# Convolution layers 2 and 3 on row groups without halos: 64x64 and 32x32 products that join each group and its next

## The chip, the cores and the metric

The kernel runs on one core of one Trainium2 chip. The metric is the device time in microseconds (us) of one execution of the whole kernel. The engines are TensorE (PE, with PEld for its weight loads), VectorE (DVE), ScalarE (ACT), GpSimd (POOL) and SyncE (SP, which only issues DMAs). Each engine works through its own instructions in order and waits on semaphores for the others.

## The reference

Four residual layers act on x of shape (4, 8, 512, 512), float32. Each adds a branch of the group-normalised input, with 4 groups of 2 channels.

```python
x = x + _L0_conv_ref(_gn(x), ...)            # spiking attention with four projections
x = x + _L1_conv_ref(_gn(x), L1_conv_w)      # depthwise 13x13, reflected edges
x = x + _L2_conv_ref(_gn(x), L2_conv_weight, L2_conv_bias)
x = x + _L3_conv_ref(_gn(x), L3_conv_weight, L3_conv_bias)
```

The change concerns layers 2 and 3, both 3x3 convolutions from 8 to 8 channels with a border of zeros. Layer 2 rounds its input and its weights to integers of at most 127 before it convolves (the scale of the input is the largest absolute value of the whole normalised tensor), and divides by the scales afterwards. Layer 3 is a plain float32 convolution.

```python
sx = MAX_Q / jnp.max(jnp.abs(x))
qx = jnp.clip(jnp.round(x * sx), -MAX_Q, MAX_Q)      # the weights likewise, with sw
out = conv(qx, qw, padding=1) / (sx * sw) + bias     # layer 2
out = conv(x, weight, padding=1) + bias              # layer 3
```

The four images along the first axis are called t = 0 to 3 below; an image has 8 channels of 512 rows.

## The kernel before

Layers 0 and 1 come first and leave their result in DRAM, one tensor `x2d[t]` for each image. Its rows are image row by image row with the 8 channels of a row side by side, so that consecutive partitions hold row 0 channel 0, row 0 channel 1 and so on. Inside a row the 512 columns are stored by phase: first every fourth column from 0, then every fourth from 1, and so on (`PH` = 4 phases of `NV` = 128 columns). Layer 1 needed that order and layer 2 works in it: a step of one column is a step to the next phase, and only the outer two phases need a neighbour from another phase, which the padded tile `xq` of six phases holds.

Layers 2 and 3 (`layers23`) cut each image into 85 windows of 8 rows (`W_IN`), one every 6 rows (`W_STEP`). A window is 64 partitions, a tile two windows, a pair two tiles; an image has 22 pairs. The work of one step of the loop at the end is one pair:

- `load` brings a pair from DRAM, five steps ahead, with two DMAs on SP's queue.
- `normalise` (L1113, ACT) scales and shifts it, two steps ahead. `quantise` (L1125, DVE) rounds it to bf16 integers one step ahead, and POOL fills in the two padding phases (L1129, L1130).
- `layer2` runs three 128x128 products of 512 columns per tile (L1146, PE), one for each horizontal tap. `band2` holds the vertical taps as a banded matrix, with two corner blocks by which the two windows of a tile serve each other. DVE (L1153) takes the sum out of PSUM, scales it, adds the residual and writes it to `x3` in the natural order of columns, so with a step of four floats. ACT squares some tiles for the statistics of layer 3's group norm (L1160), DVE does the others (L1165).
- `halos` copies the rows at the windows' edges between the windows in `x3` by DMA (L1304), in four chunks per image and pair of windows, on SP's queue for the first image and on POOL's for the others.
- `norm3` makes the mean and deviation of the finished image and folds them into the weights `band_t`. It is a generator that is resumed twice a step, so that its pieces lie between the others. A mask leaves the windows' doubled rows out of the sums.
- `layer3` works on the image before, 22 + `LAG` = 25 steps behind layer 2. Each window takes three 64x64 float32 products (L1249, PE; each is two records in the profile); the four windows of a pair lie in four different quarters of the array. The residual is folded into the middle tap. ACT adds a constant and takes the result out of PSUM (L1258), and one DMA per tile on SP's queue stores 12 rows (L1265). Four banks of PSUM (`ps_r`) serve it, two per step.

The order on each engine is set by a scheduler, with hints: `tc.issue_after(op)` places what follows behind `op`. `weights23` builds the banded matrices out of the taps with short products (L951) while layer 1 runs. `x3` is a ring of 26 pairs.

Of the kernel before, what the change touches and what calls it, by code (L numbers as in the profile page):

```python
# [67 lines left out]
W_IN, W_STEP, W_ALL = 8, 6, 85  # L68
N_PAIRS = (W_ALL + 3) // 4
W2_N = 2 * N_PAIRS - 1  # L70
HALF = P // 2
LAG = 3
RING = 23 + LAG


def place(q):

    p, c = divmod(q, 4)
    return p, c // 2, (c % 2) ^ (c // 2)


def windows(k):

    p, j = divmod(k, 2)
    every = [(a, 4 * p + 2 * j + (a ^ j)) for a in range(2)]
    return [(a, q) for a, q in every if q < W_ALL]


def valid(q):

    return 0 if q == 0 else 1, W_IN if q == W_ALL - 1 else W_IN - 1
# [6 lines left out]
def shape_constants():  # L98
# [3 lines left out]
    mask2 = np.zeros((2, W_IN, B, W2_N, 2), np.float32)  # L102
    for k in range(W2_N):
        for a, q in windows(k):
            mask2[a, slice(*valid(q)), :, k] = 1
# [9 lines left out]
    for o in range(W1_OUT):  # L115
# [3 lines left out]
    c128 = np.concatenate(  # L119
        [block, same, ind, mask2.reshape(P, -1), eye.reshape(P, -1)], 1  # L120
    )

    c24 = np.zeros((3, B, 2 * W_IN + 1, B), np.float32)
    for dy in range(3):
        c24[dy, np.arange(B), W_IN - 1 + dy, np.arange(B)] = 1
    return c128, slide.reshape(K1, -1), c24.reshape(3 * B, -1)
# [3 lines left out]
def network(ctx: ExitStack, tc: tile.TileContext, i: dict, out: bass.AP):  # L130
# [19 lines left out]
    block, same, ind = part(P), part(P), part(G)  # L150
    mask2 = part(W2_N * 2)
# [58 lines left out]
    st1 = [const.tile([P, T, PAIR, NC, 2, 6], F32, name=f"st1_{g}") for g in range(G)]  # L210
# [14 lines left out]
    shared = first.enter_context(tc.tile_pool(name="shared", bufs=1))  # L225
    with ExitStack() as s:
        head = layer0(
            s, tc, i, x_in, x1d, ident, block, avg, group_stats, st1, norm1, band1d, r1, w_sum, shared
        )
# [3 lines left out]
    def pool(name, bufs=1, **where):  # L233
# [3 lines left out]
    st2 = late.tile([P, T, B, W1_N // 2 // N_PS1, 6], F32, name="st2")  # L237
# [4 lines left out]
        "x": ctx.enter_context(pool("x2", 9, side="right")),  # L242
        "y": ctx.enter_context(pool("y2", 2, side="right")),
        "o": ctx.enter_context(pool("o3", 10, side="right")),
    }
    with ExitStack() as s:
        ps_1 = s.enter_context(pool("ps_2", space=PSUM))
        layer1 = Layer1(
# [3 lines left out]
        for g in range(1, G):  # L252
            if g == 1:
                with ExitStack() as behind:
                    for op in layer1.started:
                        behind.enter_context(tc.issue_after(op))
                    norm1(G - 1, ps_1)
                    w23 = weights23(tc, i, late, early["y"], ps_1, ident)
# [3 lines left out]
    with ExitStack() as s:  # L262
        layers23(
            s, tc, x2d, out, ident, ind, mask2, avg_same, group_steps, m2, r2, most, w23, early, pool
        )
# [655 lines left out]
def weights23(tc, i, pool, scratch, ps_1, ident):  # L921
# [7 lines left out]
    n_taps = 3 * B  # L929
    w = {}  # L930
    parts = scratch.tile([P, 2, D], F32, tag="y", name="parts")
    c24 = parts[:n_taps, 0, : i["c24"].shape[1]]
    nc.scalar.dma_start(c24, i["c24"])
    w2, w3, below = (parts[:n_taps, 1, j * n_taps : (j + 1) * n_taps] for j in range(3))
    nc.scalar.dma_start(w2, i["w2"])
    nc.scalar.dma_start(w3, i["w3"])
    inner = parts[:, 1, P : P + 3 * HALF // 2].bitcast(BF16)
# [6 lines left out]
    def banded(taps, band, name, firsts):  # L944

        for b, first in enumerate(firsts):
            ps = ps_1.tile([P, W_IN, n_taps], F32, tag="misc", name=f"ps_{name}")
            for row in range(W_IN):
                at = (W_IN - first - row) * B
                for a in range(2):  # L950
                    nc.tensor.matmul(  # L951
                        ps[a * HALF : (a + 1) * HALF, row, :], lhsT=c24[:, at : at + HALF],
                        rhs=taps, start=True, stop=True,
                    )
            for dx in range(3):
                nc.vector.tensor_copy(
                    band[:, b, dx, :].rearrange("p (r c) -> p r c", c=B),
                    ps[:, :, dx * B : (dx + 1) * B],
                )
        return band  # L960

    band3 = pool.tile([P, 2, 3, HALF], F32, name="band3")
    w["band3"] = banded(w3, band3, "band3", (-1, 1))
    w["sum3"] = pool.tile([P, 2, HALF], F32, name="sum3")
    nc.vector.tensor_add(w["sum3"], band3[:, :, 0, :], band3[:, :, 1, :])
    nc.vector.tensor_add(w["sum3"], w["sum3"], band3[:, :, 2, :])
    w["eye3"] = pool.tile([P, 2, 3, HALF], F32, name="eye3")
    nc.vector.memset(w["eye3"], 0.0)  # L970
    nc.vector.tensor_add(
        w["eye3"][:, 0, 1, B:], ident[:, : HALF - B], ident[:, HALF : P - B]
    )
    nc.vector.tensor_add(
        w["eye3"][:, 1, 1, : HALF - B], ident[:, B:HALF], ident[:, HALF + B :]
    )

    wall = scratch.tile([P, 2, D], F32, tag="y", name="wall")
# [12 lines left out]
    w["band2"] = band2 = pool.tile([P, 2, 3, P], BF16, name="band2")  # L991
    nc.gpsimd.memset(band2, 0.0)
    inner = banded(w2, inner.rearrange("p (b x m) -> p b x m", b=1, x=3), "inner2", (0,))
    nc.vector.tensor_copy(below, w2)
    nc.vector.memset(below[: 2 * B, :], 0.0)
    ps = ps_1.tile([P, 2, n_taps], F32, tag="misc", name="ps_outer2")
    for a in range(2):
        half = slice(a * HALF, (a + 1) * HALF)
        at = (W_IN - W_STEP) * B
# [348 lines left out]
```

## Time and profile before

| what | value |
|---|---|
| median of 3 runs | 2902.83 us (2902.46 to 2903.03) |
| span of the profiled execution, first to last instruction | 2900.8 us |
| PE busy | 2818.8 us, 97% of the span |
| DVE, POOL, ACT busy | 2183.1, 868.8, 549.2 us |
| layers 2 and 3 | from about 2492 us to the end |
| layer 2 products (L1146) | 516 records, 131.5 us busy |
| layer 3 products (L1249) | 2040 records, 242.7 us busy |
| loads of layer 2, stores of layer 3 | 168 of 256 KB, 164 of 192 KB |

The profiled execution has no time of its own beside its span; the span is 2.0 us below the median of the runs. A group line in the profile names the source line, engine, operation, output<-inputs and shapes, then the count, the busy time and the mean length of one instruction; what follows is the idle time of the engine just before them and what ended it. Matmuls overlap, so their busy time is less than count times mean. A line of the chain of waits gives a start, a length and the instructions that the end of the program hung on in that stretch.

### The profile page before, as it was taken

The page shows a single profiled execution, that of the slowest core. Times are in us where ns is not written, and L with a number is a line of the kernel's source. Part 1 is how long each engine was busy: PE and PEld are TensorE (multiplying, and loading weights), DVE is VectorE, ACT ScalarE, POOL GpSimd, SP SyncE. Part 2 cuts the span into 40 slices and gives each one's busy share as a digit, 9 for nine tenths or more (in the row PEclk, how much of TensorE's full clock was granted, in tenths as well). Part 3 has the DMA queues.
Part 4 walks back from the last instruction along what each step waited for, and adds up shares of the span by engine and source line. Part 5 has one row for each costly group of instructions (what it writes and reads, how often), then busy time and mean ns, then how long its engine had stood idle before and what let it go on. Part 6 is the DMA issues. An engine that isn't in the chain of part 4 may idle for free. (4 is left out here: it accounts for less than half of the span.)

```text
span 2900.8 us, 36559 instructions
## 1 busy us (share of the span) xinstructions
PE 2818.8 (97%) x12868; PEld 1302.5 (45%) x12868; DVE 2183.1 (75%) x3888; ACT 549.2 (19%) x851; POOL 868.8 (30%) x1920
## 2 busy tenths in 40 slices
PE   7999999999999999999999999999999999689999
PEld 3444555545555545455555555445333333223334
DVE  6897788788779878878877886886665665888870
ACT  2200100011010001001000000110111121677774
POOL 2242243333234323333422343332311111232220
PEclk9899999999999999999999999999999999999999
DMA  8433222223222232222222122212877788699975
GB/s 209 115 89 76 59 67 67 74 74 74 59 67 67 77 76 68 59 67 67 75 67 51 45 59 52 52 45 75 221 203 207 209 219 224 157 201 234 224 191 148
DMA packets 326127, 324.01 MB, mean 112 GB/s; under 512 B 21519, under 2 KB 240439, under 8 KB 325831
## 3 DMA queue, kind: packets, MB, share of 16 engines
q1 hardware_dynamic: 263024, 239.48, 34.1%
q0 software_dynamic: 19776, 56.14, 6.0%
q10 hardware_dynamic: 43143, 26.05, 3.1%
q8 instruction: 101, 1.65, 0.3%
q14 instruction: 83, 0.68, 0.1%
HBM read 212.44 MB, written 103.65 MB: 109 GB/s over the span
## 5 line engine op out<-in xcount | busy, mean ns | idle before, releaser
L524 PE MATMUL ps_in<-w_v,xn 128*128 128x512 f32 x1024 | 459.1, 599 | 5.4 <-DVE w_v L359 5.4
L524 PE MATMUL ps_in<-w_kq,xn 128*128 128x512 f32 x1024 | 449.8, 592 | 0.0
L843 PE MATMUL ps_conv<-x,bt 112*64 112x512 f32 x2048 | 445.2, 592 | 0.1
L524 PE MATMUL ps_in<-xn,w_kq 128*128 128x512 f32 x1024 | 444.9, 592 | 0.0
L560 PE MATMUL ps_b<-toep,vtok 128*64 128x512 bf16 x3072 | 367.1, 383 | 0.4 <-DVE v_o L575 0.4
L475 ACT ACTIVATE h_q<-v_q,c_half 128x512 f32<-128x512 f32 x96 | 69.1, 721 | 1473.6 <-DVE v_q L471 893.9
L500 POOL TENSOR_TENSOR h_v<-h_v,c_v 128x512 f32<-128x512 f32 x96 | 121.8, 1269 | 728.0 <-DVE h_v L499 700.1
L587 PE MATMUL ps_out<-wp,so 128*128 128x512 f32 x1024 | 308.7, 444 | 0.0
L609 POOL COPY x1s<-x1s 128x2 f32<-128x2 f32 (+1 forms) x1024 | 226.6, 275 | 273.0 <-DVE x1s L598 273.0
L524 PEld LDWEIGHTS ps_in<-xn,w_kq 128*128 128x128 f32 x1024 | 194.3, 190 | 232.5 <-issue 220.4
L524 PEld LDWEIGHTS ps_in<-w_kq,xn 128*128 128x128 f32 x1024 | 194.3, 190 | 220.7 <-issue 206.2
L524 PEld LDWEIGHTS ps_in<-w_v,xn 128*128 128x128 f32 x1024 | 191.4, 191 | 222.9 <-issue 212.1
L843 PEld LDWEIGHTS ps_conv<-x,bt 112*64 112x64 f32 x2048 | 146.5, 135 | 288.0 <-issue 286.0
L560 PEld LDWEIGHTS <-vtok 128*64 128x64 bf16 x3072 | 176.1, 111 | 155.1 <-issue 5.6
L1249 PE MATMUL ps_conv<-x,band_t 64*64 64x512 f32 x2040 | 242.7, 595 | 0.0
L587 PEld LDWEIGHTS ps_out<-wp,so 128*128 128x128 f32 x1024 | 192.6, 188 | 94.0 <-issue 57.8
L1153 DVE SCALAR_TENSOR_TENSOR x<-ps_conv,inv,x 128x512 f32<-128x512 f32 (+1 forms) x172 | 186.1, 1169 | 46.9 <-PE ps_conv L1146 46.7
L598 DVE SCALAR_TENSOR_TENSOR x1s<-v_p,xr 128x256 f32<-128x256 f32 x256 | 187.6, 773 | 14.6 <-DMA x<-x1s 3.8
L865 POOL DMA_DIRECT2D x<-xo x128 | 71.4, 564 | 330.6 <-ACT xo L850 316.3
L850 ACT ACTIVATE xo<-ps_conv,off 128x512 f32<-128x512 f32 x128 | 87.6, 687 | 430.6 <-PE ps_conv L843 307.4
L500 POOL TENSOR_TENSOR h_k<-h_k,c_k 128x512 f32<-128x512 f32 x96 | 122.0, 1270 | 138.4 <-DVE h_k L499 138.4
L1146 PE MATMUL ps_conv<-xq,band 128*128 128x512 bf16 (+1 forms) x516 | 131.5, 391 | 31.3 <-POOL xq L1129 31.3
(193 smaller groups left out, 3113.8 us busy)
## 6 DMA issues: line engine op xcount, KB each, us to landing
x<-x SPq DMA_DIRECT2D x64, 917.0 KB
x<-x SPq DMA_DIRECT2D x168, 256.0 KB
x<-x1s POOLq DMA_DIRECT2D x128, 262.0 KB, 2.7
xq<-in_x SPq DMA_DIRECT2D x128, 256.0 KB
xr<-in_x SPq DMA_DIRECT2D x128, 256.0 KB
out<-o SPq DMA_DIRECT2D x164, 192.0 KB
xs<-in_x SPq DMA_DIRECT2D x112, 256.0 KB
x<-xo ACTq DMA_DIRECT2D x128, 128.0 KB
```

The lines of the kernel that those rows point to most:

```text
L500: nc.gpsimd.tensor_add(h, h, c_twice[n])
L524: mm = nc.tensor.matmul(ps, lhsT=lhsT, rhs=rhs, start=k == 0, stop=k == NC - 1)
L560: nc.tensor.matmul(pb[two * DH : (two + 1) * DH, :], lhsT=v[:, c, h * DH : (h + 1) * DH], rhs=toep[z][:, h, u : u + N], start=c == 0 and z ...
L587: nc.tensor.matmul(ps, lhsT=so[:, k, c * P : (c + 1) * P], rhs=wpT[z][:, k, :], start=k == 0 and z == 0, stop=k == NC - 1 and z == 1,)
L598: nc.vector.scalar_tensor_tensor(own, v.rearrange("p (g v) -> p g v", g=PH)[:, two, :], 1.0, by_phase[:, two, :], op0=ALU.is_ge, op1=ALU.add,)
L609: nc.gpsimd.tensor_copy(x1[:, f, u : u + n], x1[:, fm, um - n + 1 : um + 1][:, ::-1])
L843: mm = nc.tensor.matmul(ps[q * M1 : (q + 1) * M1, :], lhsT=bt[:, z, :], rhs=xt[:, w0 : w0 + N_PS1, z : z + NV], start=z == 0, stop=z == SH ...
L850: nc.scalar.activation(xo[:, a, :], ps, AF.Identity, bias=off[:, t : t + 1])
L865: engine.dma_start(bass.AP(dst.tensor, dst.offset + (q * n_half * W1_OUT * B + b) * D + f * NV, [[B * D, W1_OUT], [W1_OUT * B * D, n_half] ...
L1146: mm = nc.tensor.matmul(ps[:n_p, :], lhsT=w["band2"][:n_p, j, dx, :n_p], rhs=xq[:, j, dx : dx + PH, :], start=dx == 0, stop=dx == 2,)
L1153: done["DVE"] = nc.vector.scalar_tensor_tensor(own.rearrange("p (v g) -> p g v", g=PH), by_phase(ps[:n_p, :]), w["inv"][:n_p], by_phase(x[ ...
L1249: mm = nc.tensor.matmul(ps[j][b * HALF : (b + 1) * HALF, :], lhsT=band[half, b, dx, :], rhs=x3[half, s0 + j, dx : dx + D], start=dx == 0, ...
```

## The change

The windows go. An image is cut into 32 tiles of 16 rows (`W2_N` = 32); a tile is two octets of 8 rows (64 partitions) for layer 2 and four quads of 4 rows (32 partitions) for layer 3. A step of the loop prepares a pair of tiles, so an image has 17 steps (`N_PREP` = 17, the last of which has half a tile).

Layer 2: the input octet o holds rows 8o to 8o+6 and, in its last eight partitions, row 8o-1. Its output octet, rows 8o to 8o+7, then needs only its own input octet and the next one. So each output half takes three 64x64 products from its own input (opening) and three from the next (closing), and those of a tile are issued beside the opening ones of the tile after. The row that the eight partitions should hold for the residual, 8o+7, is loaded over row 8o-1 by two more DMAs on ACT's queue once `normalise` has read the tile. The DVE eviction reads and writes in phase order without a step; `x3` keeps six phases with padding, which POOL fills.

Layer 3: an output group is 4 rows, shifted by one row against the quads, so that it needs two quads, q and q+1: three 32x32 float32 products from each. The opening products of one step and the closing ones of the step before are issued together, and every one of the sixteen has its own 32x32 tile of the array. A step works on one bank of groups from the upper part of the image and one from the lower part. ACT's eviction now also undoes the phases: it reads PSUM with a step of 128 floats. A store is 16 rows.

A one-column product (`token`) stands after the first opening products and after the last closing ones, in both layers. The order on PE is the order of the program text (`tc.manual_schedule`). The mask and the halo copies go; the pools of x and o buffers shrink (9 to 7, 10 to 6), the statistics buffers `st1` and `st2` move to other pools, and the ring `x3` has 43 tiles.

The diff, cut to its core:

```diff
-W_IN, W_STEP, W_ALL = 8, 6, 85
-N_PAIRS = (W_ALL + 3) // 4
-W2_N = 2 * N_PAIRS - 1
-HALF = P // 2
+OCT, QUAD = 8, 4
+HALF, QP = P // 2, P // 4
+W2_N = N // W2_ROWS
+N_PREP = W2_N // 2 + 1
+N_3 = W2_N // 2 + 1
 LAG = 3
-RING = 23 + LAG
+RING = W2_N + 2 * LAG + 5
...
-        "x": ctx.enter_context(pool("x2", 9, side="right")),
+        "x": ctx.enter_context(pool("x2", 7, side="right")),
...
-        "o": ctx.enter_context(pool("o3", 10, side="right")),
+        "o": ctx.enter_context(pool("o3", 6, side="right")),
...
+    band3 = pool.tile([P, 2, 4, QP], F32, name="band3")
+    banded(into3, w3, QUAD, band3, "band3")
...
+    w["band2"] = band2 = pool.tile([P, 3, 3, HALF], BF16, name="band2")
+    banded(into2, w2, OCT, band2, "band2")
+    nc.vector.tensor_scalar_mul(band2[:, 2], band2[:, 0], inside)
...
     def load(t, p):
...
+        for a in range(2):
+            end = (a + 1) * HALF
             nc.sync.dma_start(
+                xt[a * HALF : end - B, :, :], rows_of(t, first + a * OCT, 2, HALF - B)
             )
+            j = 1 if p == 0 and a == 0 else 0
+            nc.sync.dma_start(
+                xt[end - B : end, j:, :],
+                rows_of(t, first + a * OCT - 1 + j * W2_ROWS, 2 - j, B),
+            )
...
     def normalise(t, p):
...
+        if p < N_PREP - 1:
+            for a in range(2):
+                end = (a + 1) * HALF
+                nc.scalar.dma_start(
+                    x[end - B : end, :, :],
+                    rows_of(t, 2 * p * W2_ROWS + (a + 1) * OCT - 1, 2, B),
+                )
...
+    def token(size):
+        ps = ps_1.tile([P, 1], F32, tag="misc", name="token")
+        own = w["band2"][:size, 0, 0, :]
+        return nc.tensor.matmul(
+            ps[:size, :], lhsT=own[:, :size], rhs=own[:, :1], start=True, stop=True
+        ).ins
+
+    def products2(ps, t, k, dx, last):
+        halves = [slice(a * HALF, (a + 1) * HALF) for a in range(2)]
+        for a, half in enumerate(halves):
+            kind, j, b = 0, k, a
+            if last:
+                kind, j, b = 1, k + a, 1 - a
+            elif k == 0 and a == 0:
+                kind = 2
+            xq = ready[t, j // 2][1]
+            mm = nc.tensor.matmul(
+                ps[half, :], lhsT=w["band2"][halves[b], kind, dx, :],
+                rhs=xq[halves[b], j % 2, dx : dx + PH, :],
+                start=dx == 0 and not last, stop=dx == 2 and last, skip_group_check=True,
+            )
+        return mm
...
     def layer2(t, p):
+        for k in (2 * p, 2 * p + 1) if p < N_PREP - 1 else (W2_N,):
+            if k < W2_N:
+                open2[k] = ps_2.tile([P, D], F32, tag="conv2", name="ps_conv2")
+            for dx in range(3):
+                if k < W2_N:
+                    mm = products2(open2[k], t, k, dx, False)
+                if k > 0:
+                    if dx == 0:
+                        token(HALF)
+                    mm = products2(open2[k - 1], t, k - 1, dx, True)
+            token(HALF)
+            if k > 0:
+                evict2(t, k - 1, open2.pop(k - 1))
...
+    def evict2(t, k, ps):
...
+        done["DVE"] = nc.vector.scalar_tensor_tensor(
+            inner, ps, w["inv"], x, op0=ALU.mult, op1=ALU.add,
+            accum_out=sums[:, 0, :] if summed else None,
+        ).ins
...
+        nc.gpsimd.tensor_copy(own[:, 0, 1:], own[:, PH, : NV - 1])
+        nc.gpsimd.tensor_copy(own[:, PH + 1, : NV - 1], own[:, 1, 1:])
...
+    def products3(banks, n, dx, last):
+        t, i = divmod(n, N_3)
+        band = norms[t][1]
+        for ps, quads in zip(banks, banks3(i)):
+            for q, c in quads:
+                src, g = quad_of(t, q + last)
+                mm = nc.tensor.matmul(
+                    ps[c * QP : (c + 1) * QP, :],
+                    lhsT=band[g * QP : (g + 1) * QP, int(last), dx, :],
+                    rhs=src[:, dx : dx + PH, :],
+                    start=dx == 0 and not last, stop=dx == 2 and last, skip_group_check=True,
+                )
+        return mm
...
     def layer3(n):
...
         for dx in range(3):
+            if n < T * N_3:
+                mm = products3(open3[n], n, dx, False)
+            if n > 0:
+                if dx == 0:
+                    token(QP)
+                mm = products3(open3[n - 1], n - 1, dx, True)
+        token(QP)
+        if n > 0:
+            evict3(*divmod(n - 1, N_3), open3.pop(n - 1))
...
+    def evict3(t, i, banks):
...
+                nc.scalar.activation(
+                    o[a:b].rearrange("p (v g) -> p v g", g=PH),
+                    ps[a:b].rearrange("p (g v) -> p v g", g=PH), AF.Identity, bias=const[a:b],
+                )
...
+    n_all = T * N_PREP
...
+    with tc.manual_schedule(engines={mybir.EngineType.PE}):
+        for n in range(n_all + N_3 + LAG + 1):
...
```

In the last stretch, `banks3(i)` lists the groups of a step (quad q, column quarter c): up to four from the upper bank and four from the lower one. `quad_of` finds a quad's ring tile and its quarter of the partitions, or a constant pad outside the image. `norm3` loses the mask, sums the constant of four quarters instead of two halves and fills the pad tile on POOL.

## The prediction

> **What bounds the kernel now.** I read the engines' busy time first, then the stages, then the chain of waits inside the stage that is changed, and last the prices of single instructions.
>
> ```profile
> PE 2818.8 (97%) x12868; PEld 1302.5 (45%) x12868; DVE 2183.1 (75%) x3888; ACT 549.2 (19%) x851; POOL 868.8 (30%) x1920
> ```
>
> PE is busy nearly throughout. Layers 2 and 3 run from 2492 us to the end, so 409 us are at stake; the rest is touched only by the weight setup. Busy time by stage (then granted clock, DMA share, GB/s):
>
> ```profile
> core 0: us, PE busy (x) PEld busy (x) DVE busy (x) ACT busy (x) POOL busy (x), PEclk, DMA share, GB/s
> 2492.00:2569.00 77.00, 43.17 (x161) 17.14 (x160) 71.46 (x149) 63.28 (x116) 21.52 (x57) 0.87 0.81 158
> 2569.00:2636.00 67.00, 66.36 (x482) 21.28 (x480) 54.28 (x85) 50.50 (x83) 22.00 (x66) 1.00 0.95 240
> 2662.00:2720.00 58.00, 58.00 (x425) 18.63 (x428) 45.76 (x72) 43.88 (x71) 18.38 (x59) 1.00 0.95 248
> 2828.00:2896.00 68.00, 67.63 (x593) 32.84 (x585) 5.00 (x16) 33.77 (x50) 5.27 (x26) 1.00 0.57 154
> ```
>
> There are three stages. Layer 2 alone (77 us) is bound by DVE and ACT. The mixed stage, layer 2 of one image beside layer 3 of the one before (2569 to 2828, 259 us, 63 steps), and layer 3 alone (68 us) are bound by PE. The chain that ended last says the same:
>
> ```profile
> 2677.19 1.40 PE ps_conv L1146 x6
> 2678.59 2.74 PE ps_conv L1249 x24
> ...
> 2838.68 54.03 PE ps_conv L1249 x498
> ```
>
> A mixed step is 1.40 + 2.74 = 4.14 us of PE with no wait between. In the last stage 54.03 / 498 x 24 = 2.60 us make a step, so a round of four 64x64 records lasts 0.434 us and a change of stage inside a step about 0.14. The timeline of ACT in the mixed stage, and of its normalising in layer 2 alone:
>
> ```profile
> 2680.32 0.72 ACT L1160 ACTIVATE square<-x,m_own 128x512 bf16<-128x512 f32 x1 [1.13 <-DVE x L1153]
> ...
> 2681.04 1.23 ACT L1113 ACTIVATE y<-x,mr_own,r_own 128x1024 f32<-128x1024 f32 x1
> 2682.18 1.24 ACT L1258 ACTIVATE o<-ps_conv,const 128x512 f32<-128x512 f32 x2
> 2684.42 0.72 ACT L1160 ACTIVATE square<-x,m_own 128x512 bf16<-128x512 f32 x1 [1.01 <-ACT o L1258]
> ...
> 2515.34 1.23 ACT L1113 ACTIVATE y<-x,mr_own,r_own 128x1024 f32<-128x1024 f32 x1
> ...
> 2517.95 1.22 ACT L1113 ACTIVATE y<-x,mr_own,r_own 128x1024 f32<-128x1024 f32 x1
> ```
>
> Start to start, ACT's mixed step is square 0.72, normalise 1.14, two evictions 1.24: 3.10 of 4.14 us. In layer 2 alone the period is 2.61. Prices of accesses and of DMA issues (minimum/median/maximum ns where three stand):
>
> ```profile
> L1153 DVE SCALAR_TENSOR_TENSOR x<-ps_conv,inv,x 128x512 f32<-128x512 f32 x168 | 181.4, 1169 | 46.9 <-PE ps_conv L1146 46.7
> ...
> L492 DVE SCALAR_TENSOR_TENSOR v_p<-h_p,ps_out 128x512 f32<-128x512 f32 x8 | 5.5, 683 | 3.6 <-PE ps_out L587 3.6
> ...
> L617 ACTq DMA_DIRECT2D x<-x1s x192: 221/263/361, 118.2 to 2031.1; - x192
> ...
> L865 ACTq DMA_DIRECT2D x<-xo x128: 540/695/2117, 2049.8 to 2486.5; - x128
> ```
>
> L1153 writes with a step of four floats, L492 without: 1169 against 683 ns.
>
> [...] This trace shows four 64x64 tiles fully concurrent (0.434 us a round) and nothing at 32x32. [...]
>
> **The change, part by part.**
>
> *PE work.* An image falls from 22 steps to 17. Layer 3 has 129 groups of 4 rows, six products each, spread over 16 tiles: still six rounds a step, 6 x 0.434 + 0.14 = 2.74. Layer 2 has two tiles a step, three rounds each of four 64x64 products: 6 x 0.21 + 0.14 = 1.40, as now. So 5 x 4.14 = 21 us an image would go. Added are the tokens, two in layer 3 and four in layer 2. A token uses a tile that already has two records queued, so what is behind it in PE's order waits between 0 and one round (0.43). I take 0.25 in layer 3 and 0.2 in layer 2: blocks of 3.0 and 1.6, a PE step of 4.6.
>
> *Layer 3's banks.* Now two banks are in use and two are being evicted, a step apart. After the change a bank stays open for two steps, so all four are taken, and the next step's first products wait for evictions that start only when this step's last products end. Queued behind them on PE are the closing products, though these could run. In the mixed stage layer 2's 1.6 us covers 1.6 of it; in the last stage nothing does.
>
> *The eviction* moves the undoing of the column phases from DVE to ACT, which now reads PSUM with a step of 128 floats. Bounds: 0 (two evictions 1.24) to +0.49 each (L1153 less L492). I take +0.45: two evictions 2.15, with 0.15 to start, 2.3.
>
> *DVE* falls from 1169 to about 700 ns a tile (L492). In the mixed stage it is off the path; in layer 2 alone ACT was level with it, so no time is gained.
>
> *ACT issues* two DMAs a step for the rows that shared a partition. Each waits for the normalising, and squares and evictions stand behind it. Bounds for an issue: 0.26 (L617, one row) to 0.70 (L865, 256 pieces); I take 0.5, and 0.1 for the wait: 1.1. ACT's mixed step becomes 3.10 + 1.1 + 0.9 = 5.1 us.
>
> *SP* issues four loads and two stores a step instead of two and two: a load's issue has a median of 0.62 us (L1096) and a least of 0.49, a store's 0.81 (L1265, 12 rows) to 0.87 (13 rows), so a step takes 3.6 to 4.2 us, below 5.1 and hidden; if ACT and PE came down to 4.2, SP would be next. *Bytes*: an image loads 512 rows of 8 channels by 2 KB, 8.39 MB, and 64 of the rows again, 1.05 MB, and stores 8.39 MB: per step 1.05 MB, against 1.01 MB (two loads of 256 KB, two stores of 192 KB, halos) in 4.14 us; at the 248 GB/s of the table 4.2 us, hidden likewise. *Halo copies* go, 1.3 POOL issues of 0.6 us a step; POOL gets four pad copies of at most 0.4 and two small ones: 2.8 with layer 2's own, covered.
>
> *Small things.* Weight setup goes from 104 to 128 short records inside layer 1, where PE is full: the trace has 32 in 1.11 us, so +0.8. The masks' two DVE passes go and a pad fill comes, within the three steps that layer 3 lags. PE's order is now written out, so the group sums stand in it and PE may wait for DVE: 0 to 6 us an image, I take 3. Fewer buffers for x and o: loads still run five steps ahead, nothing; moved statistics buffers: nothing.
>
> *Sum.* Layer 2 alone: 16 steps of 1.14 + 1.1 + 2 x 0.74 = 3.7, a half step 1.5, three steps of the next image 3.0, start and norm 8: 78 (was 77). Mixed: 48 steps; PE and ACT meet at the eviction, 3.0 + 2.3 = 5.3, ACT alone 5.1; I take 5.2: 250, plus two norms 6, less the short steps 3: 253 (was 259). Last stage: 20 steps of 5.1 (3.0 + 2.3, less a little where the first bank is free early) and a closing 1.5: 103.5 (was 68). So 434.5 against 404, with setup +31 us. The profiled execution has only its span, 2900.8 us; the median of the runs is 2902.8, 2.0 more. Span 2932; **2934 us** in terms of the median.
>
> **The rivals.**
>
> *Faster: the stepped PSUM read costs nothing.* The two evictions with their start take 1.4 us and hide under layer 2's 1.6; PE sets 4.6, ACT 4.2. Mixed 221 + 3, last 20 x 4.4 + 1.5 = 89.5, layer 2 alone 76: 389.5, time 2889. With free tokens and issues of 0.26: 4.3 a step, 4.1 last, 72: 2867. It decides below about 0.25 us extra per eviction. For it: ACT's evictions are among its cheapest operations; against: DVE pays 0.49 for a step.
>
> *Slower still: the 16 tiles do not all run together.* At 12 of 16 a layer-3 block is 3.9 us, a mixed step 6.1, the last ones 6.0: 78 + 296 + 121 = 495, time 2995; at 8 of 16 about 3090. For it: no record here is 32x32, and a step of layer 3 has 96 records instead of 24, so PE must be fed four times as fast; against: the four 64x64 tiles are perfectly parallel.
>
> *Transfers become the bound.* DMA share is 0.95 now[...]: 4.2 us a step at today's rate, 5 at a sixth less: 2905 to 2945.
>
> That the change does not do what it says would be the second rival.
>
> **How the numbers follow.** The forecast's case 0.50 (its own range 2908 to 2965), faster 0.27 (2867 to 2896), tiles not concurrent 0.12 (2975 to 3090), transfers 0.11. A measurement of this kernel can tell about 0.2% from no change, 6 us. Faster by more 0.27, within 0.08, slower 0.65. The range, 2868 to 2990, leaves out most of the second rival and the edge of the first.
>
> **What would show it.** Layer 3's MATMULs as 32*32, a block of about 3 us; evictions near 1.1 us instead of 0.67; PE waiting at layer 3's first products for ACT's evictions, above all after layer 2 has ended; ACT over 90% busy with its issues. Evictions of 0.7 us, or PE never waiting for ACT, would make the forecast wrong towards faster; blocks over 3.5 us towards slower.

## The result, and the profile after

| | before | after |
|---|---|---|
| median of 4 runs each | 2902.64 us (2902.36 to 2903.03) | 2922.41 us (2920.26 to 2925.77) |
| span of the profiled execution | 2900.8 us | 2920.9 us |
| layer 2 alone | 74 us | 72 us |
| mixed stage | 259 us, steps of 4.14 | 251 us, steps of 5.34 |
| layer 3 alone | 68 us, steps of 2.60 | 99 us, steps of 4.74 |

The ratio after to before is 1.0071, with a 95% interval of 1.0057 to 1.0086: slower, by 20 us, against 31 in the forecast. Almost nothing is gained or lost ahead of layer 2, whose first product starts at 2495 us in the one profile and at 2494 in the other.

The busy line of the page after:

```profile
PE 2830.2 (97%) x18509; PEld 1350.1 (46%) x18509; DVE 2079.7 (71%) x3772; ACT 490.2 (17%) x745; POOL 909.2 (31%) x2143
```

PE is as full as before and DVE and ACT have less to do, so an average over the program says nothing of the cause. The stages do. (In what follows a block is what PE does for one layer in one step, timed from its first record to the first of the next block; a record is one instruction in the profile, and a float32 product is two records.) Busy time by stage of the kernel after (then granted clock, DMA share, GB/s):

```profile
2494.00:2566.00 72.00, 47.34 (x579) 24.01 (x583) 46.99 (x117) 50.00 (x90) 43.11 (x152) 0.80 0.57 145
2566.00:2636.00 70.00, 68.68 (x1569) 32.82 (x1564) 37.12 (x68) 41.06 (x65) 25.84 (x84) 1.00 0.71 199
2669.00:2721.00 52.00, 51.46 (x1241) 25.08 (x1226) 26.70 (x48) 31.07 (x49) 19.04 (x61) 1.00 0.75 209
2817.00:2916.00 99.00, 84.04 (x1998) 37.79 (x1996) 4.86 (x23) 27.98 (x46) 5.74 (x36) 1.00 0.38 113
```

The first column after the window is its length, the second PE's busy time. In the mixed stage PE is busy for 51.46 of 52 us, and the DMA share has fallen from 0.95 to 0.75: PE bounds it. In layer 3 alone PE stands still for 15 of 99 us. The costliest groups of the kernel after, by shape:

```profile
L1267 PE MATMUL ps_conv<-x,band_t 32*32 32x512 f32 x6144 | 247.0, 597 | 14.7 <-ACT o L1308 14.7
L1131 PE MATMUL ps_conv<-xq,band 64*64 64x512 bf16 x1536 | 133.6, 407 | 27.5 <-DVE x L1168 14.5 <-POOL xq L1103 13.0
...
L1168 DVE SCALAR_TENSOR_TENSOR x<-ps_conv,inv,x 128x512 f32<-128x512 f32 x128 | 95.2, 749 | 119.1 <-PE ps_conv L1131 116.6 <-DMA x<-x 2.4
L1308 ACT ACTIVATE o<-ps_conv,const 128x512 f32<-128x512 f32 x124 | 78.6, 683 | 141.5 <-issue 65.2 <-PE ps_conv L1267 64.9 <-DMA x<-x 5.8
```

L1308 is the eviction with the stepped read of PSUM. It takes 683 ns; the forecast wanted 1.1 us, and before it was about 0.67. L1267 waits 14.7 us for it all the same, and DVE's eviction fell from 1169 to 749 ns. One mixed step on PE, then on ACT:

```profile
2687.63 0.62 PE L1131 MATMUL ps_conv<-xq,band 64*64 64x512 bf16 x4
...
2687.87 0.81 PE L1131 MATMUL ps_conv<-xq,band 64*64 64x512 bf16 x9
2688.33 0.16 PE L1116 MATMUL token<-band 64*64 64x1 bf16 x1
2688.36 0.38 PE L1131 MATMUL ps_conv<-xq,band 64*64 64x512 bf16 x1
2688.80 0.16 PE L1116 MATMUL token<-band 64*64 64x1 bf16 x1
2688.80 0.83 PE L1131 MATMUL ps_conv<-xq,band 64*64 64x512 bf16 x10
2689.27 0.16 PE L1116 MATMUL token<-band 64*64 64x1 bf16 x1
2689.57 1.26 PE L1267 MATMUL ps_conv<-x,band_t 32*32 32x512 f32 x32
2690.48 0.16 PE L1116 MATMUL token<-band 32*32 32x1 bf16 x1
2690.64 2.40 PE L1267 MATMUL ps_conv<-x,band_t 32*32 32x512 f32 x64
2692.64 0.16 PE L1116 MATMUL token<-band 32*32 32x1 bf16 x1
2692.97 0.62 PE L1131 MATMUL ps_conv<-xq,band 64*64 64x512 bf16 x4
```

```profile
2690.32 1.23 ACT L1078 ACTIVATE y<-x,mr_own,r_own 128x1024 f32<-128x1024 f32 x1
2691.58 0.63 ACTq L1085 DMA_DIRECT2D x<-x  x2
2693.01 1.26 ACT L1308 ACTIVATE o<-ps_conv,const 128x512 f32<-128x512 f32 x2 [1.46 <-PE ps_conv L1267]
```

From start to start, the layer-2 block takes 1.94 us (2687.63 to 2689.57) and the layer-3 block 3.40 (to 2692.97), where the forecast had 1.6 and 3.0. The two evictions begin 0.04 us into the next layer-2 block and are over before it ends, and ACT waited 1.46 us ahead of them: ACT is not the bound. In layer 3 alone, where nothing stands between two steps of layer 3, PE does wait for them. Its timeline there, and the two waits of the whole profile for evictions (total, times, longest):

```profile
2839.43 2.31 PE L1267 MATMUL ps_conv<-x,band_t 32*32 32x512 f32 x44
2841.17 0.16 PE L1116 MATMUL token<-band 32*32 32x1 bf16 x1
2843.09 1.73 PE L1267 MATMUL ps_conv<-x,band_t 32*32 32x512 f32 x36 [1.36 <-ACT o L1308]
...
2847.83 1.73 PE L1267 MATMUL ps_conv<-x,band_t 32*32 32x512 f32 x36 [0.76 <-ACT o L1308]
```

```profile
PEld ps_conv L1267 <- ACT o L1308: 39.8, 50, 2.3
...
PE ps_conv L1267 <- ACT o L1308: 14.7, 21, 1.4
```

A step there takes 4.74 us (2843.09 to 2847.83); against the block of 3.40 that is 1.34 us of waiting.

### The profile page after: what moved, and what is told of

It is laid out like the page before. It is cut to its first block, busy times and chain, and to the rows that moved or that the text cites. A ratio compares the mean times of both kernels' runs of the same rounds, so it can differ in the third digit from the quotient of the medians.

```text
span 2920.9 us, 47801 instructions
## 1 busy us (share of the span) xinstructions
PE 2830.2 (97%) x18509; PEld 1350.1 (46%) x18509; DVE 2079.7 (71%) x3772; ACT 490.2 (17%) x745; POOL 909.2 (31%) x2143
## 5 line engine op out<-in xcount | busy, mean ns | idle before, releaser
L1267 PE MATMUL ps_conv<-x,band_t 32*32 32x512 f32 x6144 | 247.0, 597 | 14.7 <-ACT o L1308 14.7
L1168 DVE SCALAR_TENSOR_TENSOR x<-ps_conv,inv,x 128x512 f32<-128x512 f32 x128 | 95.2, 749 | 119.1 <-PE ps_conv L1131 116.6
L1131 PE MATMUL ps_conv<-xq,band 64*64 64x512 bf16 x1536 | 133.6, 407 | 27.5 <-DVE x L1168 14.5
```

The lines of the kernel that those rows point to most:

```text
L1131: mm = nc.tensor.matmul(ps[half, :], lhsT=w["band2"][halves[b], kind, dx, :], rhs=xq[halves[b], j % 2, dx : dx + PH, :], start=dx == 0 and ...
L1168: done["DVE"] = nc.vector.scalar_tensor_tensor(inner, ps, w["inv"], x, op0=ALU.mult, op1=ALU.add, accum_out=sums[:, 0, :] if summed else None,
L1267: mm = nc.tensor.matmul(ps[c * QP : (c + 1) * QP, :], lhsT=band[g * QP : (g + 1) * QP, int(last), dx, :], rhs=src[:, dx : dx + PH, :], sta ...
```

## The experiments

Three theories were tried. **A**: the excess of both blocks comes from the tokens, and the last stage's wait from the banks. **B**: small records set the blocks, whatever the tokens do. **C**: ACT paces the last stage. A was later narrowed to A2 and B to B2. Two more were added for the block of layer 3: **D**, a limit on how many records may be under way over all tiles, and **E**, neighbouring tiles that hold each other up.

**More banks in the last stage** (on the changed kernel): the second bank of a step comes out of layer 2's pool. That pool has three banks, so seven go round in place of four, one more than the expectation says.

```diff
-            open3[n] = [
-                ps_3.tile([P, D], F32, tag="conv3", name="ps_conv3") for _ in banks3(i)
-            ]
+            pools = [(ps_3, "conv3"), (ps_3, "conv3")]
+            if n >= n_all - N_3 - LAG:
+                pools[1] = ps_2, "conv2"
+            open3[n] = [
+                own.tile([P, D], F32, tag=tag, name="ps_conv3")
+                for (own, tag), _ in zip(pools, banks3(i))
+            ]
```

> Edit: once layer 2 has ended, layer 3 takes one of its two banks of a step from layer 2's pool, so that six banks go round instead of four. Theory A (PE is held by the two evictions, because all banks are open or being evicted): a step of the last stage falls from 4.74 us by the 1.34 us wait to the block's own 3.4, 19 such steps are 25 us, the mixed stage keeps its 5.34 us a step: 2897 us, under the 2902.6 of the kernel before. Theory C (the last stage is paced by ACT's work or by the output buffers and stores behind it): steps stay at 4.6 to 4.74 us and the time at 2918 to 2922 us.

2900.17 us, ratio to before 0.9992 (0.9983 to 1.0). The last stage takes 75.1 us instead of 98.6, its step 3.39, and the waits are gone:

```profile
PEld ps_conv L1267 <- ACT o L1312: 5.6, 16, 0.4
...
PE ps_conv L1267 <- ACT o L1312: 0.2, 1, 0.2
```

The wait was for banks, as theory A said, and C falls. This alone brings the change back to the time of before.

**Tokens on another tile** (on the changed kernel).

```diff
-            ps[:size, :], lhsT=own[:, :size], rhs=own[:, :1], start=True, stop=True
+            ps[P - size :, :], lhsT=own[:, :size], rhs=own[:, :1], start=True, stop=True
```

> Edit: every token uses the tile in the last column of the array (rows 0, columns 96 to 127 or 64 to 127) instead of tile (0, 0); number, place in PE's order and waits are the same. Theory A (a token sits in the queue of the tile that the next product needs first, and what is behind that product waits, with all 16 tiles idle): the layer-3 block falls from 3.40 to 3.0 to 3.15 us, the layer-2 block from 1.94 to 1.5 to 1.7, 48 mixed steps gain 0.45 to 0.8 each and the 20 last ones 0.25 to 0.4: 2876 to 2896 us. Theory B (the blocks are long because 96 small records cannot be fed or do not all run together): blocks stay within 0.05 us, 2919 to 2923 us.

2921.28 us, ratio 1.0066 (1.0051 to 1.0081). The blocks are 1.94 and 3.40 us, as before the edit. Theory A in this form falls: what a token costs does not depend on the tile it uses.

**Both edits.**

> Edit: the two edits together. Theory A: the gains add, as the wait for the banks and the wait behind the tokens are different ones: 25 us from the last stage, 26 to 46 from the tokens, 2850 to 2871 us. Theory B: the gain of the banks alone, 2895 to 2899 us.

2901.0 us, ratio 0.9997 (0.9988 to 1.0005): the banks' gain alone.

**Two more tokens in each layer-3 step** (on the changed kernel).

```diff
-                if dx == 0:
-                    token(QP)
+                token(QP)
```

> Edit: layer 3 issues a token in each of its three stages of a step instead of the first alone, two more a step on tile (0, 0), as now. Theory A: each adds what the existing one costs in the trace, 0.16 us on the tile and up to 0.3 of restart: a layer-3 block of 3.7 to 4.3 us, 68 steps, 2943 to 2983 us. Theory B: a product of one column costs nothing that can be seen, the block stays under 3.5 us and the time under 2929 us.

2929.56 us in one run, span 2927.8. Layer 2 began 2.9 us later than in the changed kernel, which this edit cannot cause; the mixed stage took 251.6 us, the last one 99.7. The layer-3 block rose to 3.47 us and the layer-2 block fell to 1.88, 0.01 us a step for two tokens (the total is 0.6 us over theory B's bound, with that late start in it). So a token is nearly free where the one before it has long been done. That left another reading. A token is a fence: in the trace it waits on a semaphore that PE's own closing products and the token before it raise, and until that has risen the products behind it in the order of the program wait too. In the run with the tokens on another tile this lies open: the first tile's last round ends as its closing token starts, and the next token and the next round start 0.28 us later:

```profile
2685.74 0.84 PE L1131 MATMUL ps_conv<-xq,band 64*64 64x512 bf16 x12
2686.41 0.44 PE L1116 MATMUL token<-band 64*64 64x1 bf16 x2
2686.69 0.83 PE L1131 MATMUL ps_conv<-xq,band 64*64 64x512 bf16 x10
```

In the changed kernel the token at 2688.80 starts with the last of four updates of that semaphore within 0.11 us (2688.690 to 2688.801), 0.47 us after the token at 2688.33 started. Theory A2 is that latency.

**The closing token moved ahead of the last closing products**, with the banks of the first experiment.

```diff
             for dx in range(3):
                 if k < W2_N:
                     mm = products2(open2[k], t, k, dx, False)
+                if dx == 2:
+                    token(HALF)
...
-            token(HALF)
```

(the same in `layer3`)

> Edit: the six banks of the first experiment, and the token that ends a layer-2 tile or a layer-3 step stands ahead of its last closing products instead of behind them; the number of tokens is the same. Theory A2 (a token's price is the latency of the one before it: the next products of the other row tiles may not be sent until the token before has come out of the array, and where two follow closely PE stands still for that time): in the layer-2 block the stop of 0.28 us between its two tiles and most of the half-filled first round of 0.21 go, 1.94 falls to 1.5 to 1.7 us; in the layer-3 block the late start of the closing products of 0.17 to 0.22 us goes, 3.40 falls to 3.2 to 3.25; 48 steps gain 0.4 to 0.65 each: 19 to 31 us under the first experiment's 2900, 2869 to 2881. Theory B2 (the small records set the blocks: how fast they can be sent and when the array takes the next round): both blocks stay within 0.05 us, 2898 to 2903.

2886.6 us, ratio 0.9942 (0.9927 to 0.9957), in neither theory's range. A timeline of PE in this run:

```profile
2686.10 0.81 PE L1131 MATMUL ps_conv<-xq,band 64*64 64x512 bf16 x9
2686.56 0.16 PE L1116 MATMUL token<-band 64*64 64x1 bf16 x1
...
2686.82 0.83 PE L1131 MATMUL ps_conv<-xq,band 64*64 64x512 bf16 x10
2687.28 0.16 PE L1116 MATMUL token<-band 64*64 64x1 bf16 x1
2687.59 1.22 PE L1268 MATMUL ps_conv<-x,band_t 32*32 32x512 f32 x32
2688.49 0.16 PE L1116 MATMUL token<-band 32*32 32x1 bf16 x1
2688.65 2.41 PE L1268 MATMUL ps_conv<-x,band_t 32*32 32x512 f32 x64
2690.66 0.16 PE L1116 MATMUL token<-band 32*32 32x1 bf16 x1
```

The second tile of layer 2 now starts at 2686.82, 0.72 us after the first one's records at 2686.10, where it was 0.93 (2687.87 to 2688.80); the layer-2 block is 1.73 us. A2 holds there, for 0.21 of its 0.28, and in layer 3 alone, where the step fell from 3.39 to 3.11. It fails for the layer-3 block of the mixed stage, still 3.41. The single records show why. A block has three groups of 16 products, one for each horizontal tap; they are called tap stages here. Starts in us from the start of the block, first and second record of a product, for the changed kernel and this one:

```
tap stage       product   changed kernel   tokens moved
1 (dx = 0)      first     0.00  0.45       0.00  0.45
                last      0.22  0.67       0.13  0.64
2 (dx = 1)      first     1.07  1.50       1.07  1.50
                last      1.37  1.82       1.37  1.82
3 (dx = 2)      second    2.12  2.57       2.12  2.57
                last      2.43  2.88       2.44  2.89
next block                3.40             3.41
```

All 16 tiles do start together, within 0.22 us, now within 0.13, and two records on one tile stand 0.43 to 0.45 us apart. But tap stage 2 begins 0.62 us after the second record of tap stage 1's first product, and tap stage 3, from its second product on, 0.62 after that of tap stage 2. This pause of about 0.19 us comes once in a tap stage, with a token in it (the first) or without (the second). So a tap stage costs about 1.04 us, not two rounds of 0.434; the 3.11 us of a step in layer 3 alone is three of them.

**No second token in layer 3 while layer 2 runs**, on top.

```diff
-            if dx == 2:
+            if dx == 2 and n >= n_all - N_3 - LAG:
                 token(QP)
```

> Edit: as the run before, and while layer 2 runs beside it layer 3 has no second token in a step (the next layer-2 token does its work). Theory A2: the first closing products of a layer-2 block then wait for the token in the first stage of layer 3, which is long out of the array; if anything is left of the half-filled first round it goes, 0 to 0.2 us a step, 0 to 10 us under the run before. Theory B2: no change, within 2 us of the run before.

2886.84 us, ratio 0.9945 (0.9928 to 0.9961), blocks 1.73 and 3.40. No change: after the fifth experiment's edit this token cost nothing more.

**A third of layer 3's products left out** (banks as in the first experiment, tokens as in the changed kernel).

```diff
-        for ps, quads in zip(banks, banks3(i)):
+        for b, (ps, quads) in enumerate(zip(banks, banks3(i))):
+            if b == 1 and dx != 1:
+                continue
...
-                    start=dx == 0 and not last, stop=dx == 2 and last, skip_group_check=True,
+                    start=dx == b and not last, stop=dx == 2 - b and last, skip_group_check=True,
```

> Edit: the six banks, and layer 3's second bank gets the products of its middle column tap alone, so 32 of the 48 products of a step are left, and half of the tiles have two records to do instead of six (the two other taps of those rows are left out). Theory B2 (the number of small records sets the block): a third fewer, the block falls from 3.40 by 0.4 to 1.1 us, to 2.3 to 3.0; 68 steps, 2825 to 2873 us. The tiles' own work as the limit (six records of 0.43 us one behind the other on the busy tiles, and the fences): the block stays at 3.2 to 3.4, 2886 to 2900 us.

2871.68 us in one run, within theory B2's range. The block in its timeline:

```profile
2690.74 0.63 PE L1269 MATMUL ps_conv<-x,band_t 32*32 32x512 f32 x4
2690.91 0.16 PE L1116 MATMUL token<-band 32*32 32x1 bf16 x1
2690.91 2.48 PE L1269 MATMUL ps_conv<-x,band_t 32*32 32x512 f32 x52
...
2693.75 0.59 PE L1131 MATMUL ps_conv<-xq,band 64*64 64x512 bf16 x4
```

3.01 us instead of 3.40, though the busy tiles still have six records each to do one behind the other. So what the tiles share, not the tiles' own work, makes up 0.4 us of the block; but the block does not shrink by the third that records alone as the limit would give.

**Layer 3's eviction in straight order**.

```diff
-                    o[a:b].rearrange("p (v g) -> p v g", g=PH),
-                    ps[a:b].rearrange("p (g v) -> p v g", g=PH), AF.Identity, bias=const[a:b],
+                    o[a:b], ps[a:b], AF.Identity, bias=const[a:b],
```

> Edit: the changed kernel, but layer 3's evictions on ACT read and write in straight order (the columns of its output stay in the order of their phases). Theory of the forecast (the stepped read of PSUM is dear on ACT, 0.45 us each): evictions of 0.67 would fall to about 0.3 and the last stage by 0.9 us a step, 18 us. Theory A and B alike (the stepped read costs nothing, as the trace has 0.68 us after against 0.67 before): evictions of 0.66 to 0.69 us, the last stage's step 4.70 to 4.75, 2919 to 2924 us.

2924.32 us in one run, last stage 98.6 us. The group of the eviction:

```profile
L1308 ACT ACTIVATE o<-ps_conv,const 128x512 f32<-128x512 f32 x124 | 78.7, 684 | 139.4 <-issue 65.2 <-PE ps_conv L1267 62.9 <-PE ps_conv L1131 5.4
```

It takes 684 ns straight and 683 stepped: the stepped read costs nothing.

**Another order in the middle tap stage**, on the fifth experiment's kernel.

```diff
+            if dx == 1:
+                mm = products3(sorted(opens + closes, key=lambda call: call[0]))
+                continue
...
```

(the rest of the edit turns the products of a tap stage into lists, so that they can be sorted)

> Edit: the fifth experiment's kernel, with the 16 products of layer 3's middle stage (the middle column tap) sent column by column of the array, the four row tiles of one column one behind the other, instead of bank by bank with the opening products first. In all runs so far the second and the third stage of a layer-3 block begin 0.61 us after the second record of the first product of the stage before began, not 0.43, and after the start the records follow at 16.6 ns. Theory D (a limit on how many records may be under way, counted over all tiles): the order makes no difference, block 3.40 us, last stage 3.1 a step, 2884 to 2889 us. Theory E (tiles that share a row or column hold each other up, so the order counts): the block changes by 0.1 us or more either way, 6 us or more in the sum over 68 steps.

2889.05 us, ratio 0.995 (0.9933 to 0.9966); block 3.40 us, last stage 71.9 us against 69.4. The mixed block does not care about the order, as theory D has it. In layer 3 alone a step rose from 3.11 to 3.22 us, which D did not have, and the total is at the edge of its range. So this run alone does not show D.

The single records of the runs go further. A tap stage is 64 instructions of PE: 16 products of two weight loads and two records. Counted in the order of the program, the record that opens tap stage 2 is the 64th behind the second record of tap stage 1's first product, with the token's two instructions in between, and it starts 0.03 us after that second record has ended (1.04 us after the start of the block by the profile, which models the ends). Tap stage 2 of the changed kernel has no token, so the count falls two instructions later: the first product of tap stage 3 starts as soon as its tile is free, at 1.92 us, and the weight load of the second is held until the same 0.03 us after the end of tap stage 2's record. With the two more tokens of the fourth experiment it is again the first product that is held, at 2.11 us in place of 1.92. In the seventh experiment, where tap stage 1 has 32 instructions and a token, the pause moves into the middle of tap stage 2, to its ninth product, at 1.07 us, once more the 64th behind. In the kernel before, a round of four tiles is 16 instructions, and no such pause is seen: the rounds follow one another at 0.43 us. All this fits a form of D with about 64 instructions of PE under way at the most, weight loads counted: an estimate from these counts, which no experiment was made to test.

**No reloading DMAs**, on the fifth experiment's kernel.

```diff
-            for a in range(2):
-                end = (a + 1) * HALF
-                nc.scalar.dma_start(
-                    x[end - B : end, :, :],
-                    rows_of(t, 2 * p * W2_ROWS + (a + 1) * OCT - 1, 2, B),
-                )
```

> Edit: the fifth experiment's kernel without the two DMAs that ACT issues in a step (the rows that share a partition with a halo row are left out of layer 2's residual). Theory of the forecast (ACT pays 0.5 us for each and waits 0.1 for the normalising ahead): ACT gains 1.1 us a step, which shows where ACT is on the path, in layer 2 alone: 16 steps, 72 to 74 us fall to 56 to 62. Theory A and D alike (the issue runs beside ACT's own instruction): layer 2 alone falls by 0 to 4 us, the mixed stage keeps its 243 within 2, 2882 to 2888 us in all.

2880.02 us in one run. Layer 2 alone 66.9 us instead of 73.8, and 70.8 to 74.4 in all runs with the reloads on ACT; mixed stage 245.2, last 69.2. Neither side hit: the DMAs cost something, in layer 2 alone only, and well under half of what the forecast put on their issues.

**The moved tokens alone**, four banks.

> Edit: the changed kernel with the moved tokens alone, four banks as there. Theory A2 and D: the mixed stage takes its 243 us as in the fifth experiment (251 in the changed kernel); in the last stage the eviction still stands between two steps, and the moved token takes away at most the late start of the closing products, 0 to 0.2 us of 4.74 a step: 97 to 99 us; 2909 to 2915 us in all. If the wait for the banks and the wait for the tokens were the same one, the last stage would fall to about 4.4 a step, 92 us.

2916.36 us in one run: mixed stage 244.5, last stage 98.4. The total is 1.4 us over the expected range, but the stages are close to what was expected: the two waits are different ones, and in the last stage the eviction hides what the tokens gain.

**The reloads on SP**, on the fifth experiment's kernel.

```diff
-                nc.scalar.dma_start(
+                nc.sync.dma_start(
                     x[end - B : end, :, :],
```

> Edit: the fifth experiment's kernel, and SP issues the two reloading DMAs of a step instead of ACT. Without these DMAs layer 2 alone took 66.9 us instead of 73.8 of the fifth experiment. If it is the place in ACT's queue that costs this (the square behind the issue waits with it): layer 2 alone at 66 to 69 us, the mixed stage as it is, 2878 to 2883 us. If it is the transfer itself (a tile's residual is late whatever queue sends it), or SP now holds the next loads behind the wait for the normalising: 72 to 77 us, 2885 to 2891.

2877.72 us (2876.89 to 2878.05, 5 runs), ratio to before 0.9916 (0.9902 to 0.9929): **the best version, 24 us under the kernel before**. Layer 2 alone took 63.0 us, less than expected. Two squares on ACT there, in the changed kernel and then in this one:

```profile
2527.50 0.71 ACT L1174 ACTIVATE square<-x,m_own 128x512 bf16<-128x512 f32 x1
2527.63 0.28 ACTq L1085 DMA_DIRECT2D x<-x  x1
...
2528.49 0.27 ACTq L1085 DMA_DIRECT2D x<-x  x1
2528.81 0.72 ACT L1174 ACTIVATE square<-x,m_own 128x512 bf16<-128x512 f32 x1 [0.51 <-DMA x<-x]
```

```profile
2525.66 0.70 ACT L1175 ACTIVATE square<-x,m_own 128x512 bf16<-128x512 f32 x1
...
2526.37 0.71 ACT L1175 ACTIVATE square<-x,m_own 128x512 bf16<-128x512 f32 x1
```

An issue takes 0.27 us and begins while ACT's own instruction still runs, so the issue is cheap. But a second issue can be late, here by 0.6 us after the first had ended, with the square queued behind it. It waits for the semaphore that its own DMA will raise too, so for an earlier DMA to land: the last update of that semaphore was at 2528.47, 0.02 us ahead of the issue at 2528.49. In the changed kernel the second issue of a pair was over 0.1 us late in 6 of the 20 pairs in layer 2 alone, 3.5 us in all, and in the fifth experiment's kernel in 7 of 20, 4.0 us. That is less than half of the 11 us between 73.8 and 63.0, and 63.0 is also under the 66.9 of the run without these DMAs. That the place in ACT's queue costs time is shown; how the rest is lost is not.

## Why the prediction was right, and where only its sum was

The direction, the range and two mechanisms held: the banks in the last stage, and transfers that stay hidden in the mixed stage. The sum of layers 2 and 3 was 434.5 us; measured are 72 + 251 + 99 = 422. Term by term:

- **The four banks**: right, shown by the first experiment. It also explains why this is the whole loss: the last stage grew by 30 us, while the two other stages together fell by 10.
- **PE's blocks**, 3.0 and 1.6 forecast, 3.40 and 1.94 measured. The step that failed is "still six rounds a step, 6 x 0.434 + 0.14 = 2.74". That sixteen 32x32 tiles, three tap stages in a row, would keep the rounds of the four 64x64 ones was the author's estimate; the trace before has nothing at 32x32. Rounds of 0.43 to 0.45 hold for a tile within a product, not from one tap stage of 16 products to the next: three tap stages at 1.04 are 3.12, and 0.28 of the 3.40 is left (in the fifth experiment's last stage, where a layer-3 step follows the one before at once, nothing is: 3.11). The sixteen tiles of the first tap stage do start together, with 6.6 ns from one start to the next in a run of records; in the two tap stages behind it that is 16.6 ns. In layer 2 "three rounds each" left out that a tile's closing products wait for a fence: records run in seven rounds of about 0.215 us, the first and last half filled, and between the two tiles PE stood for 0.28.
- **The tokens**: the allowance of 0.25 and 0.2 us rested on the wrong cause. The forecast put the cost on the tile that a token uses; moving it to another tile changed nothing, and two more per step cost 0.01 us. The cost is the wait of one token for the one before, and putting it earlier gave back 0.2 us a mixed step.
- **The stepped PSUM read**: wrong, at the lower end of its bounds. The 0.45 us was the author's estimate from DVE's 0.49, of another engine and for a step in SBUF; no trace or run shows a stepped read of PSUM to cost ACT anything (683 ns stepped, 684 straight). Two evictions take 1.27 us, not 2.15. This was what the forecast leaned on for "PE and ACT meet at the eviction": they do not. The mixed step came out at 5.34 against 5.2 because PE's blocks were 0.74 us longer than forecast, which made up for an eviction that did not matter. Evictions of 0.7 us were one of the forecast's own signs of being wrong towards faster, and ACT, to be over 90% busy, was busy for 31 of 52 us.
- **ACT's issues**, 1.1 us a step: nothing in the mixed stage. In layer 2 alone, moving them to SP saved 9 us in the medians and 11 in the profiles, 0.6 to 0.7 us for each of 16 steps. The issue, put at 0.5, takes 0.27 beside ACT's own work; the wait, put at 0.1, comes to about 0.2 a step on average (4.0 us in 20 pairs), and the rest is not accounted for. Layer 2 alone took 72 us against 78.
- **The last stage**, 103.5 forecast and 98.6 measured: a block longer by 0.4 us and a wait shorter by 0.96.
- **The faster rival** had its mechanism right, a free stepped read, and its time wrong: with PE's true blocks the mixed stage takes 251 us, not 221 + 3. Its lower end adds up to about 2865, not 2867. **The tiles that do not all run together** were nearer the truth than their weight said: all sixteen start together, but the block of 3.40 us lies almost half way from the 3.0 of the forecast to the 3.9 of that rival. (With 8 of 16 its terms give about 3110, not 3090.) **Transfers** did not bound the mixed stage, with a share of 0.75; the sixth less was the author's estimate.

Forecast and result agree to 12 us because an eviction too dear and PE blocks too cheap cancelled, and that was luck. The direction hung on it too: with the eviction at its measured price and the blocks as forecast, the sum is that of the faster rival, 2889 us. The longer blocks turned this round: against that rival the mixed stage took 27 us more, the last stage 9 more, and layer 2 alone 4 less.

## What to carry to other kernels

Price a chain of products from the distance between its stages in the records (here 1.04 us), not from one round times the number of rounds (2 x 0.434), where the trace has no tiles of that size; and price a fence by the latency of what it waits for: here an earlier place in the order cost nothing and gained 0.21 us a mixed step. Where accumulation stays open over two steps, count the banks that are open and the banks being evicted together before shrinking anything else: here seven banks going round in place of four took the last stage from 98.6 to 75.1 us. A DMA issue of 0.27 us can still be late, here by 0.6 us, and then the square behind it in ACT's queue was late with it; with the same DMAs on SP's queue the kernel took 9 us less. And where two terms of a sum could err in opposite ways, check each against the trace before trusting that the total came out.

## What was not expected of the hardware

- ACT reads PSUM with a step of 128 floats at the price of a straight read: 683 ns in the changed kernel against 684 in the eighth experiment, for 128x512 floats.
- Sixteen 32x32 float32 products in a row of tap stages take about 1.04 us a tap stage, where their two records take 0.86; the pause of 0.19 us comes with a token in the tap stage and without one, and in the mixed stage the block is 3.40 us in either order of the products. With a third of the products gone a block falls from 3.40 to 3.01 us. The instruction that is held starts 0.03 us after a record about 64 places ahead of it has ended, weight loads counted; a limit of about that many PE instructions under way is an estimate from these counts, and no experiment tested it.
- A product of one column costs 0.01 us a step for two where the one before it has long been done (fourth experiment), and 3.40 us stay 3.40 whichever tile it uses (second); but a wait for the one just before it costs 0.28 us when nothing lies between (2686.41 to 2686.69).
